# Gathering image 2's expert rows plainly and adding them on VectorE

## The chip, the cores and the metric

The kernel runs on one core of one Trainium2 chip. The metric is the device time of a whole execution in microseconds (us); a lower number is better. Times are given as the median of several runs. One further execution was recorded by the profiler; its "span" is the stretch from its first to its last instruction, and every position in time below (such as "at 1569.56") is counted from the start of that span.

The core's engines are named as the profile names them: PE (TensorE, matrix products), PEld (its weight loads), DVE (VectorE), ACT (ScalarE), POOL (GpSimd) and SP (SyncE, which issues DMAs).

## The reference

Input is x of shape (4, 32, 128, 128) in float32: four images. Two layers follow each other.

Layer 0 rearranges each image into a matrix q of 128 rows and 4096 columns (2 x 2 pixels become channels), and mixes the channels by a normalised Gram matrix:

```python
energy = jnp.einsum('bci,bcj->bij', q, q)
d = jnp.sqrt(jnp.diagonal(energy, axis1=1, axis2=2))
energy = energy / (d[:, :, None] * d[:, None, :])
attn = jax.nn.softmax(energy, axis=-1)
out = jnp.einsum('bcj,bij->bci', q, attn).reshape(B, C * R * R, h, w)
out = gamma * out + xs
```

Here `'bci,bcj->bij'` contracts over the channels, so `energy` is 4096 x 4096 for each image. It is symmetric, which the kernel uses.

Layer 1 takes each image's values as rows (tokens) of 128 numbers, applies linear attention over eight heads, and then a mixture of eight experts of which each token uses two:

```python
router_probs = jax.nn.softmax(x @ router_w + router_b, axis=-1)
top_p, top_i = jax.lax.top_k(router_probs, K)          # K = 2
top_p = top_p / jnp.sum(top_p, axis=-1, keepdims=True)
expert_out = jnp.einsum('bnd,edc->bnec', x, expert_w) + expert_b
gathered = jnp.take_along_axis(expert_out, top_i[..., None], axis=2)
return jnp.einsum('bnk,bnkc->bnc', top_p, gathered)
```

The two sublayers each begin with a layer normalisation over the 128 numbers of a token, and each result is added to its input.

## The kernel before

**One stream of PE work, and side work woven in.** The images are numbered b = 0 to 3. `attend(b, st)` is layer 0's main work of an image. It goes over pairs of column chunks of 512 (row i, column block jc, with jc up to i), and each pair takes four *steps*. A step has one product `pe` on PE (line 551), its exponential `pr` on ACT (line 554), one product `po` two steps later (line 440), and one product `pg` that uses the block's transpose (line 375). The transposes are made by DVE in 32 x 32 blocks (line 369) and by a round trip through DRAM: one DMA out (`blocks`, line 473) and six DMAs back (line 488), all issued by SP. So a step is three products of 128 x 512 in float32, each of which is two matmul records.

Everything else is written as Python generators, which the loop at lines 1333 to 1349 advances: after each half of a step, it advances those that are due. A bare `yield` is half a step; `idle(n)` is n steps in which a generator does nothing. All instructions go into the engines' queues in the order in which this loop emits them (PE, DVE, ACT and SP are scheduled by hand, and GpSimd's instructions are pinned to the program's order), and each queue is worked through in order.

**Layer 1 of images 0, 1 and 2.** It is `layer1(b, st).all_parts()`, a generator that starts when its image is 84% done and runs for the most part beside the next image's `attend`. Its parts are: `close_rows` (lines 674 to 763), which finishes layer 0 for a quarter of the tokens (row blocks kc = 0 to 3), takes each token's statistics on DVE, the inverse root on GpSimd (`pow_neg_half`, line 164, tile `rsa`), then normalises on ACT (line 639), and adds up the tokens' Gram matrix `pgram` on PE (line 671); `matrix`; `attention_rows`; and, for each half h of the tokens, `sorted_experts(h)`.

`sorted_experts` sorts the tokens by expert in DRAM so that each expert's tokens form tiles of 128:

- *Scatters* (lines 988 to 1009): GpSimd issues 32 indirect DMAs, each of which writes 128 rows `xn` to their places in `xs`. They go in pairs, one pair a step; between them are free steps. A copy of the tokens' weights (line 992) stands ahead of each 16.
- *Products* (lines 1015 to 1080): SP loads two tiles of `xs` per step (line 1022), PE transposes them (line 1063) and multiplies by the expert's weights (line 1056), both into `pys`, DVE scales the result (line 1038), and SP stores it in `ys` (line 1042).
- *Gathers* (lines 1087 to 1123): each token needs the sum of its two rows of `ys` and its value `t2`. Tokens go in groups of four columns of 128. ACT's queue fetches the group's `t2` into a tile `acc` (`fetch`, line 1092; three such tiles take turns). GpSimd then issues eight indirect DMAs (line 1107) that read 128 rows of `ys` each and add them into `acc` on the way. SP stores the finished group to the output (`put`, line 1098, four DMAs).

The gather loop for image 2 (b = B - 2) goes at two gathers a step with a free step after each four; for images 0 and 1 at one gather a step. Each gather and each pair of scatters also waits for the latest exponential (`wait_for(..., exps, ...)`), so GpSimd doesn't run ahead of the step it was emitted in. The second half's gathers start only when the first half's are all emitted (`turns`).

**Layer 1 of image 3.** It has no later image to run beside. Its `close_rows` run at the end of image 3's `attend`, as a second stream beside what image 2 still has to do; for kc = 0 it waits until image 2's products are done (`sorted`, line 687). When `attend` is at its end, lines 1357 to 1359 empty the streams that are left, image 2's first and image 3's then. `keep_running(36)` (line 744) puts 36 transposes that nobody reads ahead of the last row block's Gram matrix. After this, `last_parts` does the rest of image 3's layer 1.

Of the kernel before, what the change touches and what calls it, by code (L numbers as in the profile page):

```python
# [12 lines left out]
F32 = mybir.dt.float32  # L13
# [3 lines left out]
ALU = mybir.AluOpType  # L17
# [5 lines left out]
def kernel(  # L23
# [43 lines left out]
    nc = tc.nc  # L67
    P = 128
    B, C, H, W = x.shape
# [8 lines left out]
    NH, KQ, D = wk.shape  # L78
# [10 lines left out]
    work = ctx.enter_context(tc.tile_pool(name="work", bufs=2))  # L89
# [39 lines left out]
    def wait_for(inst, others, why):  # L129
        for other in others:  # L130
            tc.add_manual_dep(
                inst, other.name, mybir.DependencyInfo(mybir.DependencyClass.Sync, mybir.DependencyReason.DATA),
                reason=why,
            )
# [24 lines left out]
    def pinned(inst):  # L159
        tc.keep_in_program_order(inst)  # L160
        return inst
# [16 lines left out]
    def idle(n):  # L178
        for _ in range(2 * n):
            yield  # L180
# [90 lines left out]
    def tokens(ap, b):  # L271
        return ap[b].rearrange("c (s k r) w -> s r c k w", s=2, r=2)
# [84 lines left out]
    exps = []  # L357
# [239 lines left out]
    def layer1(b, st):  # L597
# [9 lines left out]
        place = stat.tile([P, 2, KT], U32, tag="place", name=f"place_{b}")  # L607
        begin = stat.tile([P, 2, NT + 1], U32, tag="begin", name=f"begin_{b}", bufs=1)
        turns = [[], []]
# [264 lines left out]
        def attention_rows(u):  # L874
# [32 lines left out]
            if u % 2:  # L907
                for _ in route(u // 2):
                    yield
                    yield  # L910
                yield
                yield
                yield from sorted_experts(u // 2)

        def sorted_experts(h):
# [12 lines left out]
            wide = work.tile([P, 2 * (pad + HR) + HR, E], F32, tag="wide", name=f"runs_{b}_{h}")  # L928
# [51 lines left out]
            ys = dram.tile([NT * P, D], F32, tag=f"ys{h}", name=f"ys_{b}_{h}")  # L980

            def offset(ap):
                return bass.IndirectOffsetOnAxis(ap=ap, axis=0)
# [4 lines left out]
            for n in range(2 * HR):  # L988
                i, k = n // HR, r0 + n % HR
                if n % HR == 0:  # L990
                    pinned(
                        nc.gpsimd.tensor_copy(xn[:, half, D:], weight[:, i, half, :].to_broadcast([P, HR, DW - D]))
                    )
                inst = nc.gpsimd.indirect_dma_start(  # L994
                    xs[h], offset(place[:, i, k : k + 1]), xn[:, k, :], None
                )
                if not scatters:
                    pinned(inst)
                else:
                    tc.declare_no_dep(inst.ins, group=f"scatter_{b}_{h}", reason="no two tokens have the same place")  # L1000
                tc.add_to_no_dep_group(f"scatter_{b}_{h}", inst.ins)
                wait_for(inst.ins, xs_made[h] + xs_read[h], "what is replaced was made and read before")
                wait_for(inst.ins, exps, "not more of these at a time than steps have")
                scatters.append(inst.ins)
                if n % 2:
                    yield
                    yield
                if n % 4 == 3 and (b < B - 2 or n % 8 == 7):
                    yield from idle(1)
            turns[h].append("moved")  # L1010
            xs_made[h][:], xs_read[h][:] = scatters, []
            yield from idle(3)
# [75 lines left out]
            accs = {}  # L1088

            def fetch(g):  # L1090
                accs[g] = work.tile([P, 4, D], F32, tag="acc", name=f"acc_{b}_{g}", bufs=3)
                nc.scalar.dma_start(accs[g], t2[:, ts(g, 4)])

            def put(g):
                for r1 in range(2):
                    for s in range(2):
                        p0 = s * 64 + r1 * 32
                        nc.sync.dma_start(dst_out[s, r1, :, ts(g, 4), :], accs[g][p0 : p0 + 32])

            groups = list(range(r0 // 4, (r0 + HR) // 4))  # L1100
            rate = 1 if b < B - 2 else 2
            fetch(groups[0])
            yield from idle(2)
            for g in groups:
                for n in range(8):
                    i, k = n // 4, 4 * g + n % 4
                    inst = nc.gpsimd.indirect_dma_start(  # L1107
                        accs[g][:, n % 4, :], None, ys, offset(place[:, i, k : k + 1]), compute_op=ALU.add
                    )
                    wait_for(pinned(inst).ins, exps, "not more of these at a time than steps have")  # L1110
                    if (n + 1) % rate == 0:
                        yield
                        yield
                    if rate == 2 and n % 4 == 3:
                        yield from idle(1)
                    if n == 3 and g != groups[0]:
                        put(g - 1)
                    if n == 3 and g != groups[-1]:
                        fetch(g + 1)
            turns[h].append("gathered")  # L1120
            yield from idle(4)
            put(groups[-1])
            yield


        dst = tokens(out, b)
        accs, tmps = {}, {}
# [189 lines left out]
    for b in range(B):  # L1317
# [15 lines left out]
        for half, _ in enumerate(chain(attend(b, states[b]), finish() if b == B - 1 else ())):  # L1333
            if half % 2 == 0:
                t = 100 * (clock[0] - start) / UNITS
                moved = []
                if closing is None and t > 84:
                    closing = layer1(b, states[b])
                    steady.append([closing.first_parts() if b == B - 1 else closing.all_parts(), clock[0]])
                for n, (steps, begin, end, count) in enumerate(timed):  # L1340
                    if t >= begin and done[n] * (end - begin) < (t - begin) * count:
                        moved.append(steps)
                        done[n] += 1
                for stream in steady:
                    if clock[0] >= stream[1]:
                        stream[1] = clock[0] + PACE
                        moved.append(stream[0])
            for steps in moved:
                next(steps, None)
# [50 lines left out]
```

## Time and profile before

| | us |
|---|---|
| median of 3 runs | 1708.62 |
| lowest and highest of them | 1706.89, 1709.43 |
| time of the profiled execution | 1708.0 |
| its span | 1706.2 |
| TensorE busy in it | 1645.4 |
| VectorE, ScalarE, GpSimd busy in it | 880.4, 927.5, 630.9 |

The profiled execution's span lies 1.8 us below its own time, and that time 0.6 us below the median of the three runs.

The profile's page gives, in this order, each engine's busy time; the span in 40 equal slices of 42.7 us with each engine's busy share in tenths and the TensorE clock that was granted; the DMA queues; the chain of work that ended last; and the costliest groups of instructions. A group's line reads: line of the kernel, engine, operation, output and input, count, busy time in all and mean length in nanoseconds, then the idle time of the engine just before these instructions and what ended most of it.

GpSimd has 192 gathers (line 1107) and 192 scatters (line 994) in all, 64 of each for each of the images 0, 1 and 2. The gathers of image 2 begin at 1453.8 and the last of them at 1605.5.

Per stretch of the span, the end looks like this (us busy in each stretch; the last column is the granted TensorE clock):

| stretch | PE | DVE | ACT | POOL | clock |
|---|---|---|---|---|---|
| 1400 to 1500 (100 us) | 100.00 | 38.46 | 52.67 | 35.51 | 1.00 |
| 1500 to 1560 (60 us) | 60.00 | 26.78 | 32.41 | 38.67 | 1.00 |
| 1560 to 1600 (40 us) | 18.97 | 16.39 | 9.63 | 33.90 | 0.80 |
| 1600 to 1640 (40 us) | 25.79 | 21.67 | 14.39 | 12.75 | 0.80 |
| 1640 to 1680 (40 us) | 37.89 | 32.55 | 36.70 | 33.35 | 0.97 |

### The profile page before, as it was taken

What the parts mean: (1) busy time and instruction counts of PE and PEld (TensorE: products, weight loads), DVE (VectorE), ACT (ScalarE), POOL (GpSimd) and SP (SyncE); (2) the same over time, 40 slices, a digit from 0 to 9 for tenths busy, and PEclk for the clock granted to TensorE, in tenths of its full rate; (3) what the DMA queues carried; (4) which work ended last, traced back from release to release, by engine and by line L of the source; (5) the groups of instructions that cost most, each with busy time, mean ns of one, the idle gap of its engine ahead of it and who ended that gap; (6) DMA issues with size and microseconds to landing.
All of it is one profiled execution on the core that took longest, in us unless ns stands there. A gap on an engine that the chain in (4) does not pass through costs nothing.

```text
span 1706.2 us, 21751 instructions
## 1 busy us (share of the span) xinstructions
PE 1645.4 (96%) x5458; PEld 876.4 (51%) x5458; DVE 880.4 (52%) x2251; ACT 927.5 (54%) x2893; POOL 630.9 (37%) x565
## 2 busy tenths in 40 slices
PE   8999999999999999999999999999999999999288
PEld 5444544455554455555554455555554455546243
DVE  4433334467485334377477334357568333346187
ACT  3555445466565555556575555556565555555076
POOL 1000000011024432454554532455555640567666
PEclk9999999999999999999999999999999999999699
DMA  4554756754458687985678676895578867993201
GB/s 133 169 178 155 208 177 212 254 178 162 164 162 261 209 248 214 250 229 148 185 216 255 229 223 215 249 251 159 166 210 240 260 213 229 236 248 63 44 12 39
DMA packets 248555, 326.53 MB, mean 191 GB/s; under 512 B 31472, under 2 KB 180080, under 8 KB 234096
## 3 DMA queue, kind: packets, MB, share of 16 engines
q1 hardware_dynamic: 206416, 285.62, 52.9%
q0 software_dynamic: 33792, 25.58, 8.5%
q10 hardware_dynamic: 8224, 13.93, 2.7%
q8 instruction: 46, 0.75, 0.2%
q14 instruction: 77, 0.63, 0.1%
HBM read 154.49 MB, written 175.80 MB: 194 GB/s over the span
## 4 chain that ended last, share of the span: by engine, by line
PE 81%; DVE 7%; ACT 4%; POOL 3%; DMA 2%; issue 2%; SPq 1%; ACTq 0%; DVEq 0%; POOLq 0%
PE po L440 23%; PE pe L551 22%; PE pg L375 19%; PE pys L1056 3%; PE py L1192 2%; PE pg L396 2%; POOL acc L1107 2%; PE pys L1063 1%; ACT xn L639 1%; PE pgram L671 1%; PE pat L797 1%; DVE df L704 1%; PE ptq L313 1%; ACT pr L554 1%; DVE F L369 1%
## 5 line engine op out<-in xcount | busy, mean ns | idle before, releaser
L554 ACT ACTIVATE pr<-pe 128x512 f32<-128x512 f32 (+1 forms) x576 | 322.3, 560 | 517.0 <-PE pe L551 429.9
L440 PE MATMUL po<-pr,qT 128*128 128x512 f32 (+3 forms) x1152 | 549.8, 559 | 3.9 <-ACT o L445 2.7
L551 PE MATMUL pe<-qn,qn 128*128 128x512 f32 x896 | 458.9, 594 | 2.0 <-ACT pr L554 1.7
L375 PE MATMUL pg<-F,qT 128*128 128x512 f32 x880 | 449.6, 592 | 0.8 <-DVE F L369 0.6
L1107 POOL DMA_INDIRECT acc<-ys,place x192 | 301.9, 1572 | 304.7 <-ACT pr L554 198.3
L369 DVE STREAM_TRANSPOSE F<-pr 128x512 f32<-128x512 f32 x440 | 306.4, 702 | 165.7 <-ACT pr L554 129.9
L440 PEld LDWEIGHTS po<-pr,qT 128*128 128x128 f32 x1152 | 214.8, 190 | 250.7 <-issue 222.2
L380 ACT ACTIVATE junk<-F 128x512 bf16<-128x512 f32 x440 | 272.8, 620 | 1.0 <-DMA F<-blocks 1.0
L375 PEld LDWEIGHTS pg<-F,qT 128*128 128x128 f32 x880 | 166.8, 190 | 195.2 <-issue 179.0
L994 POOL DMA_INDIRECT xs<-xn,place x192 | 185.6, 967 | 196.7 <-ACT pr L554 123.6
L551 PEld LDWEIGHTS pe<-qn,qn 128*128 128x128 f32 x896 | 152.6, 191 | 100.5 <-issue 93.3
L385 DVE TENSOR_TENSOR o<-o,pg 128x512 f32<-128x512 f32 x110 | 75.5, 686 | 214.3 <-PE pg L375 207.2
L1038 DVE TENSOR_TENSOR results<-pys,xn 128x256 f32<-128x256 f32 x120 | 50.1, 417 | 190.6 <-ACT xn L1032 151.7
L164 POOL TENSOR_TENSOR rn<-ss,neg_half 128x8 f32<-128x8 f32 (+1 forms) x17 | 26.9, 1582 | 321.2 <-DVE ss L325 321.2
L554 ACT ACTIVATION_READ_ACCUMULATOR pr<-pe 128x1 f32 x576 | 111.9, 194 | 0.0
L1032 ACT ACTIVATE xn<-pys 128x256 f32<-128x256 f32 x120 | 45.2, 377 | 114.9 <-PE pys L1063 95.7
L1056 PEld LDWEIGHTS pys<-ew_sb,xn 128*128 128x128 f32 x468 | 70.0, 191 | 48.4 <-issue 46.8
L551 PE MATMUL pe<-qn 128*128 128x512 f32 (+3 forms) x256 | 90.2, 435 | 0.7 <-ACT qn L344 0.7
L380 ACT ACTIVATION_READ_ACCUMULATOR junk<-F 128x1 f32 x440 | 84.4, 192 | 0.0
L639 ACT ACTIVATE xn<-T,nba,rsa 128x128 f32<-128x128 f32 x120 | 49.2, 483 | 43.5 <-POOL nba L633 43.5
L1056 PE MATMUL pys<-ew_sb,xn 128*128 x468 | 71.6, 275 | 0.0
L164 POOL TENSOR_TENSOR rsa<-dm_a,neg_half 128x8 f32<-128x8 f32 x16 | 30.1, 1881 | 112.0 <-DVE sv_a L631 111.7
(211 smaller groups left out, 1506.5 us busy)
## 6 DMA issues: line engine op xcount, KB each, us to landing
blocks<-F SPq DMA_DIRECT2D x110, 1024.0 KB
F<-blocks SPq DMA_DIRECT2D x220, 192.0 KB
F<-blocks SPq DMA_DIRECT2D x220, 128.0 KB
xn<-xs SPq DMA_DIRECT2D x114, 132.0 KB
ys<-results SPq DMA_DIRECT2D x114, 128.0 KB
F<-blocks SPq DMA_DIRECT2D x220, 64.0 KB
below<-F SPq DMA_DIRECT2D x31, 384.0 KB
out_dram<-acc SPq DMA_DIRECT2D x128, 64.0 KB
```

Source lines behind the costliest of these rows:

```text
L164: pinned(nc.gpsimd.tensor_tensor(dst, src, neg_half.to_broadcast(list(src.shape)), ALU.pow))
L369: f()
L375: nc.tensor.matmul(pg.rearrange("p (a f) -> p a f", a=4), st["qT"][i][:, ib, :], G[:, :, ib], start=(ib == 0), stop=(ib == NJ - 1),)
L380: nc.scalar.activation(junk, G[:, :, ib], AF.Copy, accum_out=st["sums"][:, NJ * i + ib, jc : jc + 1])
L385: nc.vector.tensor_tensor(o, o, pg.rearrange("p (a j c) -> p a j c", a=4, c=S), ALU.add)
L440: nc.tensor.matmul(row["po"][:, lo:hi], qT[blk // NJ][:, blk % NJ, :], w, start=start, stop=(row["left"] == 0))
L551: nc.tensor.matmul(pe[:, c0:], qn[jc][:, ts(j, P)], qn[i][:, c0:], start=True, stop=True)
L554: nc.scalar.activation(pr[:, c0:], pe[:, c0:], AF.Exp, accum_out=sums[:, t, i : i + 1]).ins
L639: nc.scalar.activation(xn[:, k, :D], T[:, k, :], AF.Identity, scale=rs[:, k, :], bias=nb[:, k, :])
L994: inst = nc.gpsimd.indirect_dma_start(xs[h], offset(place[:, i, k : k + 1]), xn[:, k, :], None)
L1056: nc.tensor.matmul(p[:, 2 * P + j * D : 2 * P + j * D + D], bufs[6 + g % 2][:, j, :D], weights[:, bass.ds(begins[2 * (g % 2) + j], D)], st ...
L1107: inst = nc.gpsimd.indirect_dma_start(accs[g][:, n % 4, :], None, ys, offset(place[:, i, k : k + 1]), compute_op=ALU.add)
```

## The change

Three things change, all of them in `sorted_experts`, and all for image 2 alone. Images 0 and 1 keep their loops (the function `gather_and_add` holds what they did).

- The scatters of image 2 lose the free step after each eight; in the second half, two free steps after the eighth and after the sixteenth scatter take their place. A pair each step remains.
- The gathers of image 2 don't add any more. They are plain (`ALU.bypass`) and write to a tile `yb` of 2 x 4 x 128 columns, one place for each of a token's two experts. They go at two a step with no free step between.
- VectorE adds the two halves of `yb` to `acc`, 512 columns at a time, two additions for each group (`combine`). `due` counts the steps: the group's `t2` is fetched one step after its first gather, the additions are emitted four steps after the step of its last gather, and the group is stored two steps later. The tile `yb` takes turns in the two buffers of the tag `wide`.

```diff
-                if n % 4 == 3 and (b < B - 2 or n % 8 == 7):
+                if b < B - 2 and n % 4 == 3:
                     yield from idle(1)
+                elif h == 1 and n in (7, 15):
+                    yield from idle(2)
...
-            rate = 1 if b < B - 2 else 2
...
+            def gather(to, g, i, j, op):
+                k = 4 * g + j
+                inst = nc.gpsimd.indirect_dma_start(to, None, ys, offset(place[:, i, k : k + 1]), compute_op=op)
+                wait_for(pinned(inst).ins, exps, "not more of these at a time than steps have")
...
+            def gather_apart():
+
+                yb = {}
+                after_steps = []
+                now = [0]
+
+                def due():
+                    now[0] += 1
+                    for at, f in [q for q in after_steps if q[0] <= now[0]]:
+                        f()
+                    after_steps[:] = [q for q in after_steps if q[0] > now[0]]
+
+                def combine(g):
+                    for i in range(2):
+                        nc.vector.tensor_tensor(accs[g], accs[g], yb[g][:, i], ALU.add)
+                    after_steps.append((now[0] + 2, partial(put, g)))
+
+                for g in groups:
+                    yb[g] = work.tile([P, 2, 4, D], F32, tag="wide", name=f"yb_{b}_{g}")
+                    after_steps.append((now[0] + 1, partial(fetch, g)))
+                    for n in range(8):
+                        gather(yb[g][:, n // 4, n % 4, :], g, n // 4, n % 4, ALU.bypass)
+                        if n == 7:
+                            after_steps.append((now[0] + 4, partial(combine, g)))
+                        if n % 2:
+                            yield
+                            yield
+                            due()
+                turns[h].append("gathered")
+                while after_steps:
+                    yield
+                    yield
+                    due()
+                yield
+                yield
+
+            yield from (gather_apart if b == B - 2 else gather_and_add)()
```

In the changed kernel the gathers' instruction is on line 1106, and the additions are on line 1141.

More of the change, by code (lines that the diff above doesn't have):

```diff
@@ L1100, in sorted_experts @@
             groups = list(range(r0 // 4, (r0 + HR) // 4))
-            rate = 1 if b < B - 2 else 2
[L1102 to L1111, printed above, removed]
+            def gather(to, g, i, j, op):
+                k = 4 * g + j
+                inst = nc.gpsimd.indirect_dma_start(to, None, ys, offset(place[:, i, k : k + 1]), compute_op=op)
+                wait_for(pinned(inst).ins, exps, "not more of these at a time than steps have")
@@ L1112, in sorted_experts, with gather_and_add @@
+            def gather_and_add():
+                fetch(groups[0])
+                yield from idle(2)
+                for g in groups:
+                    for n in range(8):
+                        gather(accs[g][:, n % 4, :], g, n // 4, n % 4, ALU.add)
                         yield
                         yield
[L1114 to L1123, printed above, removed]
+                        if n == 3 and g != groups[0]:
+                            put(g - 1)
+                        if n == 3 and g != groups[-1]:
+                            fetch(g + 1)
+                turns[h].append("gathered")
+                yield from idle(4)
+                put(groups[-1])
@@ new lines, in gather_and_add @@
+                yield
[12 more added lines that the diff above has]
+                    after_steps.append((now[0] + 2, partial(put, g)))
+                for g in groups:
+                    yb[g] = work.tile([P, 2, 4, D], F32, tag="wide", name=f"yb_{b}_{g}")
+                    after_steps.append((now[0] + 1, partial(fetch, g)))
+                    for n in range(8):
+                        gather(yb[g][:, n // 4, n % 4, :], g, n // 4, n % 4, ALU.bypass)
[5 more added lines that the diff above has]
+                            due()
+                turns[h].append("gathered")
+                while after_steps:
[3 more added lines that the diff above has]
+                yield
+                yield
```

## The prediction

> **What bounds the kernel now.** I read the page first (busy times, slices), then the busy times by stretch, the waits, and the timelines of TensorE, VectorE and GpSimd around the place where TensorE stops.
>
> ```profile
> span 1706.2 us, 21751 instructions
> PE 1645.4 (96%) x5458; PEld 876.4 (51%) x5458; DVE 880.4 (52%) x2251; ACT 927.5 (54%) x2893; POOL 630.9 (37%) x565
> ...
> PE   8999999999999999999999999999999999999288
> ...
> POOL 1000000011024432454554532455555640567666
> PEclk9999999999999999999999999999999999999699
> ...
> L1107 POOL DMA_INDIRECT acc<-ys,place x192 | 301.9, 1572 | 304.7 <-ACT pr L554 198.3
> ...
> L994 POOL DMA_INDIRECT xs<-xn,place x192 | 185.6, 967 | 196.7 <-ACT pr L554 123.6
> ```
>
> TensorE is full in 37 of 40 slices and the cut comes in one place, slice 38. In the stretches view TensorE is 99 to 100% busy up to 1575, so an edit there only permutes the same matmuls unless it makes a new gap. The gap is in TensorE's timeline:
>
> ```profile
> 1575.81 4.15 PE L186 MATMUL spare<-ident 128*128 128x128 f32 x36 [0.25 <-ACT xnT L657]
> 1609.57 3.78 PE L671 MATMUL pgram<-xn 128*128 128x128 f32 x16 [29.61 <-ACT xn L639]
> ```
>
> VectorE and GpSimd show who is late. Columns: start, length, engine, line, operation, idle before it and its releaser.
>
> ```profile
> 1578.90 0.17 DVE L631 TENSOR_SCALAR sv_a<-sv_a 128x8 f32<-128x8 f32 x1
> 1609.02 1.11 DVE L739 TENSOR_SCALAR xn<-T,rsa,nba 128x128 f32<-128x128 f32 x4 [29.96 <-POOL nba L633]
> ```
>
> ```profile
> 1567.11 1.67 POOL L164 TENSOR_TENSOR rsa<-dm_a,neg_half 128x8 f32<-128x8 f32 x1
> 1568.86 0.20 POOL L633 TENSOR_TENSOR nba<-sv_a,rsa 128x8 f32<-128x8 f32 x1
> 1569.56 1.64 POOL L1107 DMA_INDIRECT acc<-ys,place  x1 [0.50 <-issue]
> ...
> 1605.45 1.54 POOL L1107 DMA_INDIRECT acc<-ys,place  x1 [0.30 <-issue]
> 1606.43 2.27 POOL L164 TENSOR_TENSOR rsa<-dm_a,neg_half 128x8 f32<-128x8 f32 x1
> 1608.78 0.20 POOL L633 TENSOR_TENSOR nba<-sv_a,rsa 128x8 f32<-128x8 f32 x1
> ```
>
> The statistics of image 3's last rows (row block 3) are ready at 1579.07 (1578.90 + 0.17). Their inverse root is a GpSimd instruction, and it is queued behind 20 gathers of image 2, which run from 1569.56 to about 1607 one every 1.84 us (1.54 and 0.30 between two). Everything after it is a serial tail of about 97 us.
>
> [...] the granted clock is 0.50 from 1590 to 1613.5 and 1.00 from 1616. [...] a copy (L992) waited 2.56 us for scatters to land. [...] gathers beside T+df (L726, two SBUF inputs) at 1562.52 and 1575.21 took 2.62 and 2.28 us in place of 1.54. [...]
>
> **The change part by part.** The built program's instruction order gives what moves: TensorE's rows are the same set, image 2's expert matmuls (pys) come four steps earlier, and from image 3's row 7, column block 3 on its order is unchanged. On GpSimd all 64 gathers of image 2 now stand ahead of row block 1's inverse root; none is left behind row block 1, 2 or 3.
>
> *Scatters.* Eight free steps become four. Image 2's first half now needs 32 x (0.967 + 0.30) = 40.5 us, plus an inverse root (1.9) and the wait at the second copy (3), 45.5 us on GpSimd, against 16 steps of 2.71 us (before: 54.2 us from 1298.95 to 1353.14 over 20 steps), 43.4 us. GpSimd ends about 2 us late, landing adds 2.6; SP's first load of sorted rows stands 3 steps (8 us) later. Cost 0. Were that cover gone, SP would hold back the transposes' transfers queued behind it; SP stood 7.9 us at 1461.15 with TensorE still full.
>
> *Gathers.* 64 at two a step: 32 steps in place of 48. A plain gather isn't in the trace. Nearest row: the scatter, also a plain indirect move of 128 rows, 0.967. Upper bound: the adding gather, 1.572. Below 0.967 I see no reason. I take 0.97, so 1.27 with the gap. Two are 2.54 us, just under a step of three fp32 matmul pairs (3 x 0.86 = 2.58), well under one with pys (3.24). First half: VectorE's first adds, 7 steps after the first gather, stand in its order behind the transposes of pe at 1457.93, so it starts around 1437 (7 x 3.1 us earlier) and ends 16 steps of 3.1 us later, at 1487. Second half: its last pys moves from 1509.44 to the slot four steps earlier (1497.26), less early by the four pys of 0.66 us that moved ahead, so to about 1500; its ys store lands some 3 us later, so the gathers run from about 1504 to 1504 + 32 x 1.27 + 1.9 (an inverse root among them) = 1547. Row block 1's statistics come at 1558.8, block 3's at 1579: GpSimd is then free.
>
> *The wait that goes.* Row block 2 shows the undisturbed step: statistics ready 1567.11, VectorE's normalise 1569.10, 1.99 us. Block 3 then normalises at 1579.07 + 1.99 = 1581.06 instead of 1609.02: **-27.9 us**. What is late next is this chain itself (VectorE, GpSimd 1.67 us, VectorE and ScalarE, pgram); no other engine works in the gap, and SP's last outputs of image 2 at 1605 to 1611 wait for the same gathers.
>
> *Clock.* The 36 spare transposes end at 1580, pgram then starts at about 1581.6, 1.6 us later. 16 pgram matmuls took 3.78 us cold, 2.40 us at 1568.88 warm: -1.4. The stretch 1613.5 to 1616 ran at 0.75: -0.6. Together **-2.0**. Bounds: 0 to -2.5.
>
> *VectorE's 16 adds.* 128x512 with both inputs in SBUF: 0.655 us (L324), 10.5 us in all on an engine 44% busy per stretch. They stand in VectorE's queue before transposes and sums. Most fall into its waits: those of groups 4, 5, 6 before waits of 3.87, 5.58 and 4.51 us. The last pair stands between row block 1's statistics and row block 2's df, where the wait is 0.76 us and VectorE is then full down to 1579: 1.31 - 0.76 = **+0.6**. Each pair waits for gathers emitted at least 3 steps (8 us) and landed some 3 us after: no stall at 0.97. A gather beside an add may take 0.7 more: at most 16 x 0.7 = 11 us spread over 110 us of GpSimd, of which it has some 15 idle between the halves.
>
> *Row block 0* is the tight place: its inverse root follows 22 gathers of the second half, 1504.5 + 22 x 1.27 = 1532.4, statistics ready at 1533.26, and pgram has about 1.2 us to spare. I allow **+0.5** (0 to 3).
>
> *Loads and stores.* Same number; the adds' accumulator is fetched on ScalarE's queue, its buffer freed by the store four steps (10 us) before; landing took about 2.5 us (ys store 1451.5, gather 1453.79). Cost 0; were the cover gone, ScalarE's exponentials would stall behind the fetch.
>
> Sum: -27.9 - 2.0 + 0.6 + 0.5 = **-28.8 us**. The profiled execution: span 1706.2 becomes 1677.4, its time 1708.0 becomes 1679.2; against the median of 1708.62, 1679.8. I say 1679.5.
>
> **The rivals.** *Plain gathers cost 1.54.* For: both kinds read rows by index, and only scatters show 0.97. Against: the accumulate is what sets them apart. Then 22 gathers end at 1504.5 + 22 x 1.84 = 1545, row block 0's pgram comes near 1550 instead of 1538.4, TensorE gaps of about 12 us; the remaining ten end before block 1 needs GpSimd. 1679.5 + 12 = 1691.5.
>
> *Something small under the gap*[...]: 22 gathers of which six meet an add, +4 us at row block 0: 1684.
>
> *Slower: VectorE stalls at each pair of adds.* An add that waits for a late gather holds the transposes and sums queued behind it, SP's transfers of those blocks, and then TensorE. It decides from 28.8 / 8 = 3.6 us of TensorE gap per group. A group's gathers are issued by 10 us and landed by 13, and its adds stand 7 steps (18 to 22 us) after its first gather, so the landing must come over 9 us later than I think. At 12 us late beyond that on half the groups: +48, 1728. Against it: landings seen are below 4 us, with DMA engines up to 84% busy.
>
> That gathers remain at the end is excluded by the order.
>
> **How the numbers follow.** Main case 0.77 (own range 1676 to 1683), small limit 0.06, costly gathers 0.12, slower 0.05. The range 1675 to 1692 reaches over the first three. A measurement of this kernel can't tell less than 0.2% (3.4 us) from nothing: faster 0.94, same 0.01, slower 0.05.
>
> **What would show it.** L1106 gathers into yb near 0.97 us; no gather after 1550; TensorE's 29.61 us before pgram down to about 1.6, clock 1.00 through pgram; no new TensorE gap between 1430 and 1575. Wrong if VectorE waits at the adds for DMA yb<-ys, or row block 0's pgram waits on GpSimd.

## The result, and the profile after

| | before | after |
|---|---|---|
| median, us (4 runs each, in turns) | 1707.86 | 1687.58 |
| lowest and highest | 1706.89, 1709.43 | 1686.54, 1689.39 |
| span of the profiled execution | 1706.2 | 1686.1 |

The ratio is 0.9882, with a 95% interval of 0.9864 to 0.9899: 20.3 us faster. The prediction said 1679.5, within 1675 to 1692. So the direction was right, and 8 us of the gain were missing. When the same kernel was executed on two later occasions it took 1681.18 and 1692.15 us; this turned out to be the main finding, and the experiments come to it.

First what answers to the views of before. The page of after, with the span, the busy times, the slices of PE, GpSimd and the clock, and the group of plain gathers:

```profile
span 1686.1 us, 21762 instructions
...
PE 1646.6 (98%) x5458; PEld 874.7 (52%) x5458; DVE 890.3 (53%) x2267; ACT 926.6 (55%) x2893; POOL 592.2 (35%) x565
...
PE   8999999999999999999999999999999999999987
...
POOL 1000000011024442454555443344546643446166
PEclk9999999999999999999999999999999999999999
...
L1106 POOL DMA_INDIRECT yb<-ys,place x64 | 62.8, 981 | 80.2 <-DMA xn<-xs 31.8
```

The 2 in slice 38 of PE and the 6 of the clock are gone. A plain gather took 0.98 us on average. TensorE's timeline ahead of the last row block's Gram matrix, and the last statistics with their root, of after:

```profile
1585.43 4.15 PE L186 MATMUL spare<-ident 128*128 128x128 f32 x36 [0.25 <-ACT xnT L657]
1591.19 2.05 PE L671 MATMUL pgram<-xn 128*128 128x128 f32 x16 [1.61 <-ACT xn L639]
```

```profile
1588.53 0.17 DVE L631 TENSOR_SCALAR sv_a<-sv_a 128x8 f32<-128x8 f32 x1
1588.69 1.63 POOL L164 TENSOR_TENSOR rsa<-dm_a,neg_half 128x8 f32<-128x8 f32 x1 [9.96 <-DVE sv_a L631]
...
1590.64 1.12 DVE L739 TENSOR_SCALAR xn<-T,rsa,nba 128x128 f32<-128x128 f32 x4 [1.95 <-POOL nba L633]
```

The statistics are ready at 1588.70, the root starts on GpSimd within the same 0.2 us, and VectorE normalises at 1590.64: 1.94 us, where 29.95 us passed before. TensorE waits 1.61 instead of 29.61 us. But the spare transposes start at 1585.43 where they started at 1575.81: TensorE reached this point 9.6 us *later* than before, with the same matmuls done. Three places of its timeline make that up. The first (column 1 is the start, column 2 the length, the bracket the idle time before it and its releaser):

```profile
1318.54 1.02 PE L375 MATMUL pg<-F,qT 128*128 128x512 f32 x2
1319.40 1.02 PE L551 MATMUL pe<-qn,qn 128*128 128x512 f32 x2
...
1324.21 1.25 PE L440 MATMUL po<-pr,qT 128*128 128x512 f32 x2 [2.71 <-ACT o L445]
1325.25 1.91 PE L375 MATMUL pg<-F,qT 128*128 128x512 f32 x2
1326.96 1.79 PE L551 MATMUL pe<-qn,qn 128*128 128x512 f32 x2
1328.58 1.02 PE L440 MATMUL po<-pr,qT 128*128 128x512 f32 x2
```

`po` waits 2.71 us for `o`, and then two products take 1.91 and 1.79 us instead of 1.02. The busy times by stretch show the clock behind the two slow products. Columns: stretch, its length, then busy time and count of PE, PEld, DVE, ACT and POOL, then the granted clock, the DMA share and GB/s:

```profile
1320.00:1326.00 6.00, 3.29 (x8) 1.26 (x8) 3.74 (x6) 2.36 (x7) 2.61 (x3) 0.92 0.96 285
1326.00:1329.00 3.00, 3.00 (x5) 1.21 (x4) 0.04 (x1) 0.22 (x1) 2.41 (x4) 0.59 0.66 176
1329.00:1357.00 28.00, 26.82 (x72) 12.40 (x70) 9.14 (x14) 12.80 (x41) 17.87 (x20) 1.00 0.65 217
```

The granted clock is 0.59 on average between 1326 and 1329, right after TensorE stood still. The second place is a wait of 1.52 us at 1357.33, the third the end of image 2's gathers:

```profile
1544.81 1.64 PE L671 MATMUL pgram<-xn 128*128 128x128 f32 x8 [0.25 <-issue]
...
1558.05 0.55 PE L466 MATMUL ptd<-ident,pr 128*128 128x128 f32 x3 [1.43 <-issue]
```

Marks that occur once or twice in each record (the first `pe_back`, `ptd`, the spare transposes) give the sums: 6.0 us are lost by the mark at 1517 of before, another 2.6 by that at 1549, and 1.0 by 1576.

What released `o` so late? VectorE's sum and ScalarE's exponential around 1320, first of after, then of the same kernel on the second occasion:

```profile
1322.22 0.69 DVE L385 TENSOR_TENSOR o<-o,pg 128x512 f32<-128x512 f32 x1 [2.42 <-PE pe L551]
...
1322.98 0.60 ACT L554 ACTIVATE pr<-pe 128x512 f32<-128x512 f32 x1 [3.06 <-PE pe L551]
```

```profile
1319.67 0.68 DVE L385 TENSOR_TENSOR o<-o,pg 128x512 f32<-128x512 f32 x1
...
1320.43 0.60 ACT L554 ACTIVATE pr<-pe 128x512 f32<-128x512 f32 x1 [0.85 <-PE pe L551]
```

Both engines start 2.55 us later in the first record (1322.22 against 1319.67, 1322.98 against 1320.43). In the program VectorE's sum waits for nothing but the product `pg`, which TensorE's record has as done near 1319.6 in both; and the queues of all five engines hold the same instructions in the same order.

The trace also holds the times at which the products' semaphores were updated. For the four products around the wait, beside the ends in TensorE's own record (us):

| product | end, after | update, after | end, second occasion | update, second occasion |
|---|---|---|---|---|
| `pg` | 1319.56 | 1322.20 | 1319.54 | 1319.55 |
| `pe` | 1320.42 | 1322.96 | 1320.40 | 1320.41 |
| `po` | 1320.64 | 1323.00 | 1320.62 | 1320.63 |
| `pe` | 1321.50 | 1323.04 | 1321.48 | 1321.49 |

VectorE and ScalarE start 0.02 us after the updates of `pg` and of the first `pe`. So these engines aren't late by themselves: the updates are, and the last three come 0.04 us apart. On the second occasion the update of the last `pe` comes 0.86 us behind that of `po`, and both records show 1.02 us for such a `pe`. That the last `pe` was made earlier, and only its update came late, is the author's reading of these times.

The waits view shows the size of it between 1300 and 1375 (total, times, longest), first of after, then of the second occasion ("issue" is a wait whose end the record doesn't tell):

```profile
ACT pr L554 <- PE pe L551: 17.8, 12, 3.2
ACT pr L554 <- issue: 10.7, 8, 3.4
ACT pr L554 <- PE pg L375: 9.8, 3, 5.0
```

```profile
ACT pr L554 <- PE pe L551: 32.4, 28, 1.7
```

The longest waits are 5.0, 3.4 and 3.2 us on the first occasion, 1.7 on the second. Waits of this kind are called late releases below.

### The profile page after: what moved, and what is told of

Same layout as the page of the kernel before. It is cut to its first block, busy times and chain, and to the rows that moved or that the text cites. A ratio compares the mean times of both kernels' runs of the same rounds, so it can differ in the third digit from the quotient of the medians.

```text
span 1686.1 us, 21762 instructions
## 1 busy us (share of the span) xinstructions
PE 1646.6 (98%) x5458; PEld 874.7 (52%) x5458; DVE 890.3 (53%) x2267; ACT 926.6 (55%) x2893; POOL 592.2 (35%) x565
## 4 chain that ended last, share of the span: by engine, by line
PE 80%; DVE 8%; DMA 4%; ACT 3%; SPq 2%; POOL 2%; issue 2%; ACTq 0%; DVEq 0%; POOLq 0%
PE po L440 23%; PE pe L551 22%; PE pg L375 19%; PE pys L1058 3%; PE py L1231 3%; PE pg L396 2%; PE pys L1065 2%; PE pgram L671 1%; DVE df L704 1%; SPq L488 1%; DMA F<-blocks 1%; ACT xn L639 1%; PE pat L797 1%; PE ptq L313 1%; DMA blocks<-F 1%
## 5 line engine op out<-in xcount | busy, mean ns | idle before, releaser
L1106 POOL DMA_INDIRECT acc<-ys,place x128 | 201.1, 1571 | 221.8 <-ACT pr L554 179.2
L1106 POOL DMA_INDIRECT yb<-ys,place x64 | 62.8, 981 | 80.2 <-DMA xn<-xs 31.8
L164 POOL TENSOR_TENSOR rsa<-dm_a,neg_half 128x8 f32<-128x8 f32 x16 | 28.8, 1802 | 134.8 <-DVE sv_a L631 134.7
```

The source lines that it names most:

```text
L164: pinned(nc.gpsimd.tensor_tensor(dst, src, neg_half.to_broadcast(list(src.shape)), ALU.pow))
L1106: inst = nc.gpsimd.indirect_dma_start(to, None, ys, offset(place[:, i, k : k + 1]), compute_op=op)
```

## The experiments

Kernels that were executed together shared one chip and the runs of the kernel before; such a group is called an occasion here. The record gives the chip's number for the five later occasions: 14 (A), 7 (B), 10 (C), 11 and 1 (D). No chip comes twice, so what is put down to an occasion may as well belong to the chip. Ratios are to before on the same occasion. All edits are to the changed kernel.

**A, first: which part loses the 8 us?** When these four were written, the theory was that a streak of GpSimd's DMAs without free steps holds ScalarE up. `sc_pause8` gives image 2's scatters their old free steps back:

```diff
-                if b < B - 2 and n % 4 == 3:
+                if n % 4 == 3 and (b < B - 2 or n % 8 == 7):
                     yield from idle(1)
-                elif h == 1 and n in (7, 15):
-                    yield from idle(2)
```

> The changed kernel with image 2's scatters as before: in pairs, a free step after each eight, in both halves; gathers as changed. Streak theory (when GpSimd issues more than about eight indirect DMAs without a free step, ScalarE or VectorE are next released 1.5 to 5 us late, and TensorE loses 6.0 us between 1320 and 1360): no wait of ScalarE over 2 us between 1300 and 1375, TensorE's work at 1523 stands 6 us earlier, gathers begin about 4 us later (four steps more, less the 6 us), time 1681.5 us (1680 to 1683.5). Rival 'place' (the 6 us come from the loads and block stores that run there, with the DMA queues at 95% and more): the waits stay, gathers begin 10 us later, time 1687 to 1690 us.

Measured: 1680.27 us, ratio 0.9838 (0.9821 to 0.9854), no wait of ScalarE over 2 us between 1300 and 1375. It hit the number. `old_gather` keeps the new scatters and gathers as before:

```diff
+                rate = 1 if b < B - 2 else 2
...
-                        yield
-                        yield
+                        if (n + 1) % rate == 0:
+                            yield
+                            yield
+                        if rate == 2 and n % 4 == 3:
+                            yield from idle(1)
...
-            yield from (gather_apart if b == B - 2 else gather_and_add)()
+            yield from gather_and_add()
```

> The changed kernel with image 2's gathers as before: adding, four in three steps, no adds on VectorE; scatters as changed. It splits the gain. Streak theory and rival alike: the 6 us between 1320 and 1360 stay lost, as the scatters are those of the changed kernel; gathers begin at 1444 instead of 1453.8, so the stall ahead of the last pgram shrinks from 29.6 us by the 10 us that the gathers begin sooner and by the 6 us that TensorE comes later, to about 14 us; time 1697 us (1695 to 1700). Streak theory beside that: no wait of ScalarE over 2 us after 1440, as the adding gathers have a free step after each four. Rival 'fetch' (ScalarE stands behind its own fetches of residual tiles after 1520): waits of 2 us and more of ScalarE after 1440 only where a fetch is due.

Measured: 1696.69 us, ratio 0.9939 (0.9922 to 0.9955). TensorE's timeline of it ahead of the last Gram matrix:

```profile
1576.88 4.15 PE L186 MATMUL spare<-ident 128*128 128x128 f32 x36 [0.25 <-ACT xnT L657]
1598.48 3.41 PE L671 MATMUL pgram<-xn 128*128 128x128 f32 x16 [17.45 <-ACT xn L639]
```

The time is as expected, for another reason: the stall is 17.45 us and not 14, and the 6 us were *not* lost, though the scatters are those of the changed kernel. The two single changes also tell that the gains don't add: scatters alone give 11.4 us, gathers alone (`sc_pause8`) 27.8. Both shorten the same stall, and the gathers alone are enough to end it, as TensorE's timeline of `sc_pause8` shows:

```profile
1586.46 2.05 PE L671 MATMUL pgram<-xn 128*128 128x128 f32 x16 [1.59 <-ACT xn L639]
```

`ga_pause8` puts a free step after each eight plain gathers:

```diff
                         if n % 2:
                             yield
                             yield
                             due()
+                    yield from idle(1)
```

> The changed kernel with a free step after each eight of image 2's plain gathers; scatters as changed. Streak theory: ScalarE's waits of 2 to 5.6 us between 1520 and 1560 go, the 6 us between 1320 and 1360 stay; TensorE's 2.65 us of loss between 1540 and 1560 shrink to under 1; the last gather ends three or four steps later (1565 to 1567 us), ahead of row block 1's rsa; time 1685.5 us (1684 to 1688). Rival 'fetch' (ScalarE stands behind its own fetches of residual tiles, which wait for the stores of three groups before): the waits stay or grow no less, time 1687.5 to 1690 us.

Measured: 1680.06 us, ratio 0.9839 (0.9822 to 0.9855), and again nothing lost between 1300 and 1375. `all_streak` takes the free steps from the scatters of images 0 and 1 too:

```diff
-                if b < B - 2 and n % 4 == 3:
-                    yield from idle(1)
-                elif h == 1 and n in (7, 15):
+                if h == 1 and n in (7, 15):
                     yield from idle(2)
```

> The changed kernel with images 0 and 1 scattering in pairs without free steps as well. Streak theory: waits of ScalarE over 2 us, which the records of the kernels before and after don't have in these images' scatters, appear there too (2 to 4 for each image), and TensorE gains gaps and slow matmuls of up to 6 us for each image; time 1690 to 1700 us. Rival 'place': no such waits in images 0 and 1, time 1687 to 1689 us.

Measured in a single run: 1677.14 us, no new waits; 1690 us and more were expected, 13 us above that. Both expectations fell. Streaks alone do nothing on this occasion, and none of the four records has the late releases.

**B: is it the program or the occasion?** `after_again` is the changed kernel without any edit, `streak_gap` has the edits of `all_streak` and `ga_pause8`.

> The changed kernel unaltered, executed on another occasion. In the runs with a free step after each eight gathers, or with the old gathers, every queue has the same instructions and waits as the changed kernel up to 1440 us, and yet the waits of ScalarE of 3 to 5 us and TensorE's loss of 6 us between 1300 and 1375 are not in their records: the streak of scatters isn't enough to make them. Theory 'program': something that belongs to this program as a whole (where its instructions or buffers lie) makes them: the same waits at the same places, time 1687.5 us (1686 to 1690). Rival 'occasion': they belonged to the executions on that day: no wait of ScalarE over 2 us between 1300 and 1375, time 1679.5 us (1678 to 1682).

> The changed kernel with images 0 and 1 scattering in pairs without free steps as well, and a free step after each eight of image 2's gathers. Theory 'program': no rule from the order of the work; waits of ScalarE may or may not appear, 1677 to 1687 us. Rival 'streak' for what is left of it (streaks of gathers late in the program delay ScalarE, streaks of scatters don't): 1675 to 1679 us, as the run with the scatters' streaks in all images had 1677.1 us in one look, and the free steps take away TensorE's waits for F and for xn at 1484 and 1521.

Measured: `after_again` 1681.18 us (1680.27 to 1681.53), ratio 0.9849 (0.9832 to 0.9865). So the program isn't the cause by itself: the rival 'occasion' of its expectation (1678 to 1682 us) came true. `streak_gap` 1676.75 us, ratio 0.982 (0.9804 to 0.9837): 4.4 us under the changed kernel on the same occasion, and the fastest version found.

**C: a rival of the prediction, the pace, and the occasion again.** `add_two` is `old_gather` without the free step after each four, so adding gathers go at two in every step:

```diff
-                        if rate == 2 and n % 4 == 3:
-                            yield from idle(1)
```

> The changed kernel with image 2's gathers adding, as before, but two in every step as in the change; no adds on VectorE. It is the prediction's rival of costly gathers put on the chip: same order on GpSimd, 1.54 instead of 0.94 us for each. Prediction's arithmetic: 22 gathers and the gaps take 40 us from about 1505, so row block 0's root comes near 1547 and its pgram 12 us late, and nothing is behind the last rows' root: 1692 us (1688 to 1697). Rival 'order alone' (it is enough that no gather stands behind row block 1's root; what GpSimd is late by in row block 0 is covered): 1680 to 1683 us.

`plain_slow` keeps the plain gathers and VectorE's adds, but at the pace of before:

```diff
                             due()
+                        if n % 4 == 3:
+                            yield from idle(1)
```

> The changed kernel with a free step after each four of image 2's plain gathers, the pace of before (four in three steps). Eight gathers then stand between the roots of row blocks 2 and 3. Theory 'cost' (the stall is the gathers that GpSimd must still issue once the last statistics are ready): eight at 1.25 us from about 1571 end near 1581, when the last rows need the root: stall ahead of the last pgram 1.6 to 3 us, time 1680.5 us (1679 to 1684). Rival 'pace' (the two a step are what brings the gain): the stall is 10 us and more, time 1689 to 1697 us, as with the old gathers and the new scatters.

> The changed kernel unaltered, on a third occasion. If the 1687.6 us of the first occasion is how this program runs on some occasions, it comes again or not; if not, 1680.5 us (1679 to 1682.5) and no wait of ScalarE over 2 us between 1300 and 1375. Theory 'occasion' expects the second with the greater chance, 3 in 4, as none of six other executed kernels with the same order up to 1440 us had such waits.

Measured: `add_two` 1692.82 us, ratio 0.9919 (0.9902 to 0.9935); `plain_slow` 1693.63, 0.9921 (0.9904 to 0.9937); `after_third` 1692.15, 0.9908 (0.9891 to 0.9924). The late releases are back, in all three kernels, while before took 1706.64 us, as ever. ScalarE's timeline of `plain_slow`, the rows with more than 3 us of idle time between 1300 and 1350:

```profile
1310.52 0.60 ACT L554 ACTIVATE pr<-pe 128x512 f32<-128x512 f32 x1 [3.15 <-PE pe L551]
...
1323.10 0.60 ACT L554 ACTIVATE pr<-pe 128x512 f32<-128x512 f32 x1 [3.08 <-remote]
...
1342.95 0.60 ACT L554 ACTIVATE pr<-pe 128x512 f32<-128x512 f32 x1 [3.19 <-PE ptn L346]
...
1348.05 0.60 ACT L554 ACTIVATE pr<-pe 128x512 f32<-128x512 f32 x1 [3.80 <-PE pg L396]
```

They stand where after had them (1310, 1323, near 1342). On the gathers the three kernels differ, on one chip and within one group. ScalarE's timeline of `after_third`, whose gathers have no free steps:

```profile
1526.28 0.60 ACT L554 ACTIVATE pr<-pe 128x512 f32<-128x512 f32 x1 [3.70 <-PE pg L375]
...
1535.85 0.60 ACT L532 ACTIVATE pr_back<-pe_back 128x512 f32<-128x512 f32 x1 [2.97 <-PE pe_back L529]
...
1541.61 0.60 ACT L554 ACTIVATE pr<-pe 128x512 f32<-128x512 f32 x1 [4.46 <-PE pg L375]
...
1561.16 0.60 ACT L657 ACTIVATE xnT<-ptx 128x512 f32<-128x512 f32 x1 [6.47 <-remote]
```

`plain_slow`, with a free step after each four, has no wait over 2 us between 1377 and 1574. `add_two` has no such late release from its first gather of the second half up to row block 0's root either, although its gathers run without a break: they are 1.84 us apart, those of `after_third` 1.25.

So this occasion supports one half of the streak theory: where late releases occur, they occur in runs of eight and more software DMAs at 1.25 to 1.27 us, and `plain_slow`, the one kernel here with a free step after each four plain gathers, has none in its gathers.

The other half, what makes one occasion prone to them, has a sign in the traces. They fall into two kinds by the number of semaphore updates that they hold. Nine traces hold 36371 to 36444. Five hold 27863 to 29419, about a fifth less: those of before, after, `after_third`, `add_two` and `plain_slow`. Late releases stand in four of these five and in none of the nine. In the five, every update of TensorE comes within 0.08 us of its product's end until GpSimd's first indirect DMA at 502 to 503 us. Within 0.5 us of that DMA's start the first one doesn't, and of some 1577 products 173 to 214 have no update that close; it comes later or is missing. In the nine, two products at most have none. Before is the fifth: its scatters have a free step after each eight, and it has no late release between 1300 and 1375. So the late releases go with a state in which updates come late, or are missing from the trace, from GpSimd's first indirect DMA on. What makes that state, the chip or the recording itself, isn't shown: each timed run has a span and a granted clock on record, and no run shows the kernel unrecorded.

Apart from that, `add_two` puts the prediction's rival of costly gathers on the chip. TensorE's timeline at row block 0 and at the last row block:

```profile
1549.37 2.07 PE L671 MATMUL pgram<-xn 128*128 128x128 f32 x8 [6.30 <-issue]
...
1595.14 2.05 PE L671 MATMUL pgram<-xn 128*128 128x128 f32 x16 [1.60 <-ACT xn L639]
```

Row block 0's Gram matrix waits 6.30 us and its 8 products take 2.07 us, where 8 of the same size take 1.05 at 1555.57 (the granted clock was 0.89 on average between 1545 and 1575), and by the next `pgram` TensorE has lost 9.2 us there; nothing is left at the end. So the stall ahead of the last `pgram` goes with adding gathers too, if they go at two in every step. Against `after_third`, beside which it ran, `add_two` is 0.7 us slower, within the intervals of both: on this occasion the late releases of the changed kernel took about what its cheaper gathers saved. No run compares the two on an occasion without late releases. `plain_slow` shows something else. VectorE's timeline, then TensorE's:

```profile
1582.08 0.69 DVE L1141 TENSOR_TENSOR acc<-acc,yb 128x512 f32<-128x512 f32 x1 [4.08 <-DMA yb<-ys,place]
1586.71 0.69 DVE L1141 TENSOR_TENSOR acc<-acc,yb 128x512 f32<-128x512 f32 x1 [3.94 <-DMA yb<-ys,place]
1587.32 0.67 DVE L667 TENSOR_TENSOR gram<-gram,pgram 128x128 f32<-128x128 f32 x2
```

```profile
1587.66 1.11 PE L644 MATMUL ptx<-ident,xn 128*128 128x128 f32 x4 [10.28 <-DVE gram L667]
...
1597.48 2.05 PE L671 MATMUL pgram<-xn 128*128 128x128 f32 x16 [0.46 <-ACT xn L639]
```

The adds of the last groups wait 4.08 and 3.94 us for gathers that come late, the sum of the Gram matrix stands behind them in VectorE's queue, and TensorE idles 10.28 us. Its expectation counted only GpSimd's roots and fell short by 13 us, of which some 4 were lost in the late releases of the scatters. This is the prediction's "slower" rival, at a pace at which it is real.

**D: scatters with free steps, twice more, in search of a prone occasion.** `sc_pause8_b` and `sc_pause8_c` are `sc_pause8` unaltered; `both_pause8` has the edits of `sc_pause8` and `ga_pause8`.

> On two of four occasions every kernel with the changed scatters had waits of ScalarE of 3 to 5 us at 1310, 1323, 1342 and 1357, on the other two none had. This kernel, executed before on an occasion without them, has scatters with a free step after each eight and gathers without free steps; the gathers show which kind of occasion it is. Streak theory (on some occasions eight to sixteen software DMAs in a row at 1.25 to 1.27 us hold up what ScalarE and VectorE are told next), if waits of ScalarE over 3 us stand between 1510 and 1565: none between 1300 and 1375, where the scatters now pause, and the time 1682 to 1687 us. Rival 'time of the run' (it isn't the streak, on those occasions that stretch of the program is disturbed whatever is issued): waits at 1310 to 1360 here as well, time 1687 to 1693. Without waits in the gathers it is the other kind of occasion: 1680.3 us as before, and nothing is told apart.

> The changed kernel with a free step after each eight scatters and each eight gathers of image 2. Streak theory: no wait of ScalarE over 2.5 us between 1300 and 1560 on either kind of occasion; GpSimd's 64 gathers end four steps later through the scatters and three through the gathers, near 1575 to 1580, still about level with the last statistics: 1681 us (1679 to 1684). Rival 'time of the run': 1687 us and more if the run beside it shows the waits.

> Once more the changed kernel with a free step after each eight scatters, gathers without free steps; the run before fell on an occasion without waits of ScalarE in streaks. Streak theory, if the gathers' streak shows such waits (3 us and more between 1510 and 1565) this time: none between 1300 and 1375; time 1682 to 1687 us. Rival 'time of the run': waits between 1300 and 1375 too, 1687 to 1693 us. Without waits in the gathers: 1680.3 us, and the question stays open for the scatters.

Measured: `sc_pause8_b` 1680.33 us, 0.9841 (0.9825 to 0.9857); `sc_pause8_c` 1679.79, 0.9834 (0.9818 to 0.9851); no late releases in the gathers of either, so these were not prone occasions (their traces are among the nine). Whether free steps in the scatters help the changed kernel on a prone one stays open; only before's trace, with such steps, suggests it. `both_pause8` took 1684.86 us, 0.9869 (0.9852 to 0.9885), and missed: with both delays an add waits 3.20 us for its gathers, and TensorE 5.36 us for the Gram sum behind it, as in `plain_slow`.

## Why the prediction was right, and by how much

The difference to before in each stretch of the record, from marks on TensorE's timeline, beside the terms of the prediction's sum (us):

| stretch | predicted | first | second (`after_again`) | third (`after_third`) |
|---|---|---|---|---|
| up to 1517: scatters, products | 0 | +6.0 | +1.0 | +8.0 |
| 1517 to 1565: gathers, row block 0 | +0.5 | +2.6 | +1.1 | +5.9 |
| to the spare transposes | +0.6 | +1.0 | +1.0 | +1.0 |
| wait ahead of the last `pgram` | -27.9 | -28.0 | -28.0 | -28.0 |
| from there to the end | -2.0 | -1.7 | -2.8 | -2.7 |
| sum | -28.8 | -20.1 | -27.7 | -15.8 |

The sum is right to 1.1 us on the second occasion, and there the measured 1681.18 lies in the main case's own range, 1676 to 1683. On the first it doesn't: 1687.58 lies in the part of 1675 to 1692 that was there for costly gathers and a small limit, and neither came. That this number was inside is luck. The third, 1692.15, lies just outside.

- *The wait that goes*: right to 0.1 us on every occasion. The argument that the root is found free, and that one undisturbed row block shows the remaining chain, held.
- *Clock*: -2.0 against -1.7 to -2.8. The 16 products took 2.05 us, less than the 2.40 that were put in.
- *Gathers*: 0.97 taken, 0.98 measured. On the second occasion they ran from 1438.3 and ended at 1550.4; 1437 and 1547 were said.
- *Scatters, "Cost 0"*: this is the term that was mis-sized. It asked only whether GpSimd and the loads of sorted rows come too late. On the first and third occasion the late releases during the scatters took 6.0 us and some 6.1 of the 8.0 (of the rest, 1.2 is a wait for sorted rows at 1493). On the second, waits for sorted rows are left, 0.18 and 0.46 us at 1482 and 1486, of a loss of 1.0. ScalarE's timeline of before gave no warning: between 1300 and 1375 its longest idle time is 1.88 us.
- *Row block 0*, +0.5 with bounds 0 to 3: +2.6 on the first occasion, in bounds. 1.1 of it is there on the second occasion too; the other 1.5 came with late releases and not with the late root.
- *VectorE's adds*: 0.68 us each, 0.655 taken. No add waited for its gathers in the changed kernel, but on the second occasion a product `pg` at 1523.59 waited 0.72 us until an add had ended. `plain_slow` and `both_pause8` show how near that was: a few steps later, and the adds hold the Gram sum.
- *Rivals*: costly gathers were given 12 us at row block 0; 9.2 were measured with gathers of that cost. The "small limit" of 1684 was gathers that take longer beside adds; plain gathers took 0.98 us on average, adds among them, and no run puts a loss down to it. One reading was off, without consequence: 36 of TensorE's 40 slices show a 9, not 37.

How far can the late releases be explained? TensorE's record looks undisturbed while its consumers start 2.55 us later than on the second occasion. The updates' own times, in the table above, go further: VectorE and ScalarE start 0.02 us after the update, so they aren't late by themselves, and three updates 0.04 us apart don't fit products of which the last takes 1.02 us. That the updates came up to 2.6 us after the ends in TensorE's record is shown; why they did isn't.

## What to carry to other kernels

When a serial tail waits for a queue, ask what must leave that queue before the tail's own instruction, and by when; here the gathers' part alone ended the stall, and the scatters' part, which shortens the same stall, added nothing that can be seen (1680.27 us without it, 1681.18 with it, on different occasions). Moving sums from the DMA to VectorE puts waits for the DMA into VectorE's queue: none of the adds waited for its gathers in the changed kernel, and in `plain_slow`, where the gathers came some steps later, TensorE idled 10.28 us. And before a difference of half a per cent is explained by the program, execute the same program again on another occasion: here that alone moved the time by 11 us, while the kernel before stayed within 2. The count of semaphore updates in the trace told the two kinds of occasion apart.

## What the runs showed of the hardware

- Added in the DMA, a gather of 128 rows of 512 bytes took GpSimd 1.57 us (before and after); plain it took 0.98 us (after), about the 0.97 of a scatter (before).
- On two of six occasions ScalarE was released 1.4 to 4.7 us late (from the product's end in TensorE's record to the exponential's start) during runs of software DMAs at 1.25 to 1.27 us each. TensorE's semaphore updates came late there, up to 2.6 us in the case shown, and then 0.04 us apart. On the four others, runs as long passed without it, on the last two in the gathers only.
- In after, a gap of 2.71 us in TensorE's work from 1321.50 on was followed by 3.41 us at a granted clock of 0.5, from 1325.08 to 1328.49; the clock fell 0.87 us after the work had begun again. A gap of 2.77 us in `after_third` was followed by a slower stretch too (products of 1.55 and 1.91 us instead of 1.02, a granted clock of 0.95 on average between 1300 and 1329). A gap of 2.77 us at the same place in `plain_slow` was not: 1.00 was granted in that stretch. What decides it isn't shown.
